# Two graph-attention layers on one core: the order of the first group's work, and the last batch's store

## The chip, the core and the metric

The kernel runs on one core of a Trainium2 chip. A core has five engines that run beside each other and meet at semaphores: TensorE (PE, matrix products; its weight loads, PEld, are shown apart), VectorE (DVE), ScalarE (ACT), GpSimd (POOL) and SyncE (SP, which here issues the DMAs). The time is device microseconds (us) of one execution. It is given as a median over runs, and a profile of one execution shows where it goes.

## What is computed

The input `x` has 64 batches of 256 nodes with 512 features, in float32, and there is one 256 x 256 adjacency. Two layers follow, each with a norm in front and a residual behind:

```
h = relu(layernorm(x))
H = h @ W                                  # 512 -> 256
e = leaky_relu(H @ a[0] + (H @ a[1]).T, 0.2), masked by adj
x = x + concat(softmax(e) @ H, H)
h = relu(layernorm(x))
q, k, v = h @ WqT + bq, h @ WkT + bk, h @ WvT + bv     # 8 heads of 64
p = softmax(mask(q k^T / 8));   x = x + (p @ v) @ WoT + bo
```

## The kernel before

**Groups and steps.** The batches are worked in 32 groups (`g`) of two batches (`b`). Three groups are in hand at once, in stages written as Python generators. Each `next()` on a generator emits one piece of its stage. `first_norm(g)` computes the norm in front of layer 0 and turns its result into `hT0`; `first_layer(g)` is layer 0 and the second norm, which ends in `hT` and its sums; `project(g)` makes q, k and v; `scores`, `mask_pairs`, `weigh` and `outputs` are the attention of one batch. The norm's result is turned by PE for group 0. For the others DVE transposes blocks into `xt`, a DMA writes them to DRAM (`passed`), four more bring them back (`moved`), and `put` copies them into place on ACT.

**Products.** `project` and `outputs` use seven half-size products in place of eight. A product's operand can be a sum of quarters: `operand_sums` makes the sums of the data on POOL (`sums`), `weight_sums(name)` (L254) those of a weight, with four subtractions on DVE. In `project` each of q, k and v has seven pieces; the first, third and fourth product are copied from PSUM into `kept` tiles, the last into place, all by `take` (L686) on ACT, and DVE adds the others. A product that continues in the same bank can start only when the copy has read it.

**The written order.** A planner orders each engine's instructions by their dependencies and its own estimate of time. Where the text wants more, it draws edges that bind only the order on one engine: `after(instruction, name)` (L115), and `not_sooner` (L123), which puts an operation behind the one that was last written for its engine. PE's whole order is the order of the text. `take` draws such an edge for groups 0 and 1, behind whatever was last written for ACT.

**The first group.** Before the loop over groups a hand-written stretch fills the pipeline. One string (L890) gives, for each of the last nineteen of project(0)'s twenty-one pieces, numbered i = 2 to 20, what else is emitted behind it: n a piece of `first_norm`, s a piece of `first_layer(1)`. After these, each i also takes one piece of `judge()` (L283), the check that decides whether this version's bounds on the inputs hold. `judge` squares and sums weights on ACT (`squares`, L328), sums over the partitions with one product on PE (`total`), raises to powers on POOL (`norm`) and compares with small DVE operations (`test`); its verdict `wrong` is read into registers by every engine (L51). `weight_sums` comes at i = 2 (k), 8 (v) and 19 (o).

**The steps.** Each batch of each group then has a string of parts (L906, and L914 for the very first): S is its scores, m a masked head pair, u a piece of `project(g + 1)`, s of `first_layer(g + 2)`, n of `first_norm`, o of `outputs` of the batch before. In the very first step there is no batch before, and o emits nothing. At three quarters of the string `value_differences` is emitted (POOL), at half of it the residual's bias and the load of a later batch. `weigh` of a batch comes at the start of the next step.

**The end.** `outputs` adds seven products into quarters of `xt`, one DVE addition each, and then issues one store of the batch (L847).

Of the kernel before, what the change touches and what calls it, by code (L numbers as in the profile page):

```python
# [10 lines left out]
AF = mybir.ActivationFunctionType  # L11
# [46 lines left out]
def bounded(  # L58
# [224 lines left out]
    def judge():  # L283

        part = const.tile([P, 10], F32, name="part")
        vector.memset(part, 0.0)
        room = att.tile([P, 2 * HP + 1, P], F32, tag="p", name="room", bufs=1)  # L290
        heads = room[:, 2 * HP, :]
        vector.memset(heads, 0.0)
        for j in range(2):
            vector.memset(heads[j * DH : (j + 1) * DH, j * DH : (j + 1) * DH], 1.0)
        power = {}

        def bank(name):
            return mm(name).rearrange("p (h o) -> p h o", h=HP)

        for n, name in enumerate(("q", "k")):  # L300
            gram = bank(f"gram_{name}")
            for hp in range(HP):
                half, cols = hp // 2, slice(hp % 2 * P, (hp % 2 + 1) * P)
                for c in range(HP):
                    w = w_sb[name][:, c % 2, c // 2 * 2 + half, cols]
                    matmul(gram[:, hp, :], w, w, start=(c == 0), stop=(c == HP - 1))
            power[name] = room[:, n * HP : (n + 1) * HP, :]
            vector.tensor_mul(
                power[name], gram, heads[:, None, :].to_broadcast([P, HP, P])
            )  # L310
            yield
        for i in range(3):
            for n, name in enumerate(("q", "k")):
                square = bank(f"square_{name}{i}")
                for hp in range(HP):
                    a = power[name][:, hp, :]
                    matmul(square[:, hp, :], a, a, start=True, stop=True)
                if i < 2:
                    not_sooner(scalar, "copy", power[name], square)
                else:  # L320
                    scalar.activation(
                        power[name], square, AF.Square, accum_out=part[:, 8 + n : 9 + n]
                    )
                yield

        room = big.tile([P, D], F32, tag="oT1", name="squares", bufs=1)

        def squares(col, *srcs):  # L328
            sums = small.tile([P, HP], F32, tag="sums", name=f"sums{col}", bufs=2)
            for i, src in enumerate(srcs):  # L330
                to = room[:, : src.free_size()]
                if len(src.shape) == 3:
                    to = to.rearrange("p (a b) -> p a b", a=src.shape[1])
                not_sooner(
                    scalar, "activation", to, src, AF.Square, accum_out=sums[:, i : i + 1]
                )
                if src.free_size() == D and i < HP - 1:
                    yield
            vector.reduce_sum(part[:, col : col + 1], sums[:, : len(srcs)], axis=AX.X)

        yield from squares(3, *[w_sb["v"][:, :, i, :] for i in range(HP)])
        yield
        for i in range(2):
            yield from squares(i, w0_sb[:, :, i])
        yield from squares(4, bcol["q"])
        yield from squares(5, bcol["k"])
        yield from squares(6, bv_col)
        vector.reduce_max(part[:, 7:8], bad.rearrange("p a t -> p (a t)"), axis=AX.X)
        yield
        yield from squares(2, *[w0_sb[:, c, 2:] for c in range(HP)])  # L350
        yield
        for _ in range(3):
            yield
        total = mm("total")[:, :10]
        matmul(total, square_ones, part, start=True, stop=True)
        norm = const.tile([P, 10], F32, name="norm")
        vector.tensor_scalar(norm, total, 1e-30, None, op0=ALU.add)
        power = const.tile([P, 10], F32, name="power")
        gpsimd.memset(power, 0.5)
        gpsimd.memset(power[:, 7:8], 1.0)  # L360
        gpsimd.memset(power[:, 8:10], 1.0 / 32)
        gpsimd.tensor_tensor(norm, norm, power, op=ALU.pow)
        yield
        root = float(D) ** 0.5

        test = const.tile([P, 5], F32, name="test")
        side = const.tile([P, 2], F32, name="side")
        vector.tensor_add(test[:, 0:1], norm[:, 0:1], norm[:, 1:2])
        vector.tensor_scalar(
            test[:, 0:1], test[:, 0:1], root / LARGEST_SCORE, None, op0=ALU.mult  # L370
        )
        vector.tensor_scalar(side, norm[:, 8:10], root, None, op0=ALU.mult)
        vector.tensor_add(side, side, norm[:, 4:6])
        vector.tensor_mul(test[:, 1:2], side[:, 0:1], side[:, 1:2])
        vector.tensor_scalar(
            test[:, 1:2], test[:, 1:2], scale / LARGEST_SCORE, None, op0=ALU.mult
        )
        vector.tensor_scalar(
            test[:, 2:3], norm[:, 2:3], root / LARGEST_VALUE, None, op0=ALU.mult
        )  # L380
        vector.scalar_tensor_tensor(
            test[:, 3:4], norm[:, 3:4], root, norm[:, 6:7], op0=ALU.mult, op1=ALU.add
        )
        vector.tensor_scalar(
            test[:, 3:4], test[:, 3:4], 1.0 / LARGEST_VALUE, None, op0=ALU.mult
        )
        vector.tensor_scalar(test[:, 4:5], norm[:, 7:8], 2.0, None, op0=ALU.mult)
        vector.tensor_scalar(test, test, 1.0, None, op0=ALU.is_le)
        held = const.tile([P, 1], F32, name="held")
        vector.tensor_reduce(held, test, axis=AX.X, op=ALU.min)  # L390
        vector.tensor_scalar(wrong, held[0:1, :], -1.0, 1.0, op0=ALU.mult, op1=ALU.add)
        yield
# [4 lines left out]
    def stats(mv, src, t, name):  # L397
        st = small.tile([P, 6], F32, tag="st", name=f"st{name}_{t}", bufs=4)
        if vector.last:
            not_sooner(vector, "bn_stats", st, src[t])  # L400
        else:
            vector.bn_stats(st, src[t])
        vector.bn_aggr(mv[:, t, :], st)

    def norm_T(src, mv, name, by_pe):

# [16 lines left out]
        def norm(b):  # L423
            less, rstd = factor[b]
            for t in range(NT):
                r = b * NT + t
                xn[r] = att.tile([P, D], F32, tag="xn", name=f"xn{name}_{r}", bufs=2)
                operands = dict(bias=less[:, t : t + 1], scale=rstd[:, t : t + 1])
                if scalar.last:
                    not_sooner(scalar, "activation", xn[r], src[r], AF.Relu, **operands)  # L430
                else:
                    scalar.activation(xn[r], src[r], AF.Relu, **operands)

# [30 lines left out]
        def put(b, dst):  # L464
            for t in range(NT):
                to = dst[:, :, t * P : (t + 1) * P]
                if not by_pe:
                    to = to.rearrange("p c (i n) -> p c i n", n=S)
                not_sooner(scalar, "copy", to, turned[b * NT + t])

        return factors, norm, turn, fetch, put

# [63 lines left out]
    def first_layer(g):  # L536
# [99 lines left out]
            yield  # L636
        put(1, hT[:, :, N:])
        operand_sums(gpsimd, quads, sums)
        yield

    def residual(g):
# [16 lines left out]
    def project(g):  # L658
        ops = operands.pop(g)
        for name in ("q", "k", "v"):  # L660
# [24 lines left out]

            def take(to, bank, half):  # L686

                behind = [scalar.last] if g <= 1 else []
                if name == "v":
                    taken = [scalar.copy(to, bank)]  # L690
                else:
# [46 lines left out]
    def scores(g, b):  # L738
# [6 lines left out]
        for i in range(HP):  # L745
# [7 lines left out]
                    )  # L753
            pair = p[:, 2 * i : 2 * i + 2]
            for j in range(2):
                not_sooner(scalar, "activation", pair[:, j], sc[j], AF.Exp, scale=scale)
        places.extend((q_tag, k_tag))
        return p

    def mask_pairs(p):  # L760

        for i in range(HP):
# [1 line left out]
            not_sooner(  # L764
                vector, "tensor_mul", pair, pair, maskT[:, None, :, :].to_broadcast([P, 2, NT, N])
            )
            not_sooner(
                gpsimd, "tensor_add", pair[:, :, 0, :], pair[:, :, 0, :], pair[:, :, 1, :]
            )
            yield  # L770

    oTs = {}
# [36 lines left out]
    def outputs(g, b):  # L809
# [31 lines left out]
        yield  # L841
        product(second, 4, False)
        add(1, 0, second)
        yield
        product(first, 3, False)
        add(0, 1, first)
        nc.sync.dma_start(og[g, b], xt)  # L847
        yield


# [39 lines left out]
    order = "n - - - - - nss s s ss ss s s n n sn - s n".split()  # L890
    for i, parts in enumerate(order, 2):
        next(products)
        if i in (2, 8, 19):
            weight_sums("kvo"[i // 7])
        for part in parts:
            if part != "-":
                next(norms if part == "n" else pieces, None)
# [10 lines left out]
    for g in range(NG):  # L908
        products = project(g + 1) if g + 1 < NG else iter(())
        pieces = first_layer(g + 2) if g + 2 < NG else iter(())  # L910
        for b, parts in enumerate(steps):
            if g == b == 0:

                parts = "Smmnn" + parts[4:].replace("uumon", "uumnon", 1)  # L914
            if waiting is not None:
                weigh(*waiting)
                late = outputs(*waiting[:2])
            for i, part in enumerate(parts):
# [13 lines left out]
                if i == (len(parts) * 3 // 4, 6)[b]:  # L932
                    value_differences(g, b)
                if i == len(parts) // 2:
                    if b == 0 and g + 1 < NG:
                        residual(g + 1)
                    if g + 3 < NG:
# [376 lines left out]
```

## Time and profile before

| | |
|---|---|
| median of 3 runs | 2494.8 us (2494.15 to 2494.99) |
| the profiled execution | 2494.22 us; span from first to last instruction 2492.5 us, mean granted PE clock 0.998 |
| busy in the span | PE 2456.6 us (99%), PEld 2041.8 (82%), DVE 1684.7 (68%), ACT 1010.8 (41%), POOL 1017.6 (41%) |
| chain of work that ended last | PE 95%, DVE 2%, DMA 1%, ACT 1%, issue 1% |
| stores of the output | 64 of 512 KB, issued by SP; median 3.1 us from issue to landing |
| last DVE addition into the output | 2486.78 to 2487.20 us |

Such a profile comes from one execution. In rows of instructions in order of time, the first number is the start in us, the second the length; then engine, line, operation, the tile written and the tile read (a name stands for all tiles of that name), and the shapes. A bracket at the end tells how long the engine had been idle and what released it. Most operations carry L35, the line of the helper that records them, so one goes by the tiles' names: `kept_v` is a copy of v's products, `hT<-moved` is `put`, `xn` the norm's application, `r` the reciprocals of the softmax sums, `po` layer 0's weighted sum, `pq`, `pk`, `pv` the projections, `py` the output products.

### The profile page before, as it was taken

The numbers are of one execution on the slowest core, as the hardware profiler recorded it, in microseconds if no ns is written. First come the engines' busy times: TensorE is split into PE (matmuls) and PEld (weight loads), VectorE is DVE, ScalarE is ACT, GpSimd is POOL, SyncE is SP. The second block draws the span as 40 slices with busy tenths as digits, with TensorE's granted clock in tenths as the row PEclk, the third lists the DMA queues.
The fourth block names the chain that finished last, engine by engine and source line by source line (L and its number), as shares of the span: only waits on it lengthen the run. The fifth ranks groups of instructions, "written<-read, shape, count | busy, mean of one in ns | idle before, by whom it ended". The sixth has DMA issues, their size and how long they took to land.

```text
span 2492.5 us, 41319 instructions
## 1 busy us (share of the span) xinstructions
PE 2456.6 (99%) x16034; PEld 2041.8 (82%) x16034; DVE 1684.7 (68%) x3002; ACT 1010.8 (41%) x2019; POOL 1017.6 (41%) x978
## 2 busy tenths in 40 slices
PE   8899999999999999999999999999999999999998
PEld 7678888888888888888888888888888888888886
DVE  6576666767667767667766667676677666676656
ACT  5443443434443434434444344344444344343321
POOL 3433444334444334443344443344433444433332
PEclk9999999999999999999999999999999999999999
DMA  6221232322222222323222323223222223232100
GB/s 190 72 89 64 73 106 77 106 79 77 87 92 91 95 78 75 101 81 102 79 86 78 100 83 106 79 70 94 87 96 87 83 73 106 80 103 79 58 26 36
DMA packets 134809, 213.58 MB, mean 86 GB/s; under 512 B 15440, under 2 KB 79696, under 8 KB 134608
## 3 DMA queue, kind: packets, MB, share of 16 engines
q1 hardware_dynamic: 134608, 210.89, 26.3%
q8 instruction: 128, 2.10, 0.4%
q14 instruction: 73, 0.60, 0.1%
HBM read 112.20 MB, written 98.63 MB: 85 GB/s over the span
## 4 chain that ended last, share of the span: by engine, by line
PE 95%; DVE 2%; DMA 1%; ACT 1%; issue 1%; POOL 0%; SPq 0%; ACTq 0%; DVEq 0%; POOLq 0%
PE pq L137 16%; PE py L137 15%; PE pk L137 15%; PE pv L137 15%; PE sc L137 10%; PE ph L137 9%; PE pr L137 8%; PE po L137 4%; PE total L137 3%; DMA moved<-passed 0%; DVE p L35 0%; DVE r L35 0%; DMA own<-line 0%; DVE st L35 0%; DMA passed<-xt 0%
## 5 line engine op out<-in xcount | busy, mean ns | idle before, releaser
L35 POOL TENSOR_TENSOR p<-p 128x512 f32<-128x512 f32 x256 | 410.0, 1616 | 711.5 <-DVE p L35 711.5
L35 ACT ACTIVATE p<-sc 128x512 f32<-128x512 f32 x512 | 257.7, 627 | 235.7 <-PE sc L137 231.8
L35 DVE TENSOR_TENSOR p<-p,maskT 128x1024 f32<-128x1024 f32 x256 | 340.9, 1352 | 0.0
L35 DVE TENSOR_TENSOR x<-py,x 128x256 f32<-128x256 f32 x448 | 185.8, 415 | 168.7 <-PE py L137 159.5
L35 ACT ACTIVATE xn<-x,factor 128x512 f32<-128x512 f32 x256 | 194.5, 807 | 223.4 <-POOL factor L35 223.4
L35 DVE RECIPROCAL r<-total 128x256 f32<-128x256 f32 x128 | 215.6, 1726 | 90.9 <-PE total L137 90.9
L137 PE MATMUL py<-wo_sb,oT 128*128 128x256 f32 x1024 | 262.5, 380 | 1.7 <-DVE x L35 1.1
L137 PE MATMUL sc<-q,k 64*128 64x256 f32 x2048 | 252.3, 389 | 1.3 <-DVE r L35 0.8
L137 PEld LDWEIGHTS sc<-q,k 64*128 64x128 f32 x2048 | 211.1, 187 | 43.0 <-issue 26.3
L137 PE MATMUL pk<-hT,wk_sb 128*128 128x256 f32 x1024 | 244.8, 382 | 0.0
L137 PE MATMUL pv<-wv_sb,hT 128*128 128x256 f32 x1024 | 238.6, 381 | 6.0 <-ACT kept_v L35 6.0
L35 POOL TENSOR_TENSOR factor<-factor,rexp 128x2 f32<-128x2 f32 x128 | 91.5, 715 | 364.1 <-DVE factor L35 364.1
L137 PE MATMUL pq<-hT,wq_sb 128*128 128x256 f32 x1024 | 239.9, 382 | 0.0
L137 PE MATMUL ph<-w_sb,hT 128*128 128x258 f32 x1024 | 234.6, 381 | 0.3 <-ACT hT L35 0.3
L137 PE MATMUL pr<-p,v 128*32 128x256 f32 x4096 | 232.7, 379 | 0.0
L137 PEld LDWEIGHTS pv<-wv_sb,hT 128*128 128x128 f32 x1024 | 195.5, 191 | 33.2 <-ACT kept_v L35 6.8
L137 PEld LDWEIGHTS pk<-hT,wk_sb 128*128 128x128 f32 x1024 | 192.4, 190 | 35.4 <-issue 10.7
L137 PEld LDWEIGHTS pq<-hT,wq_sb 128*128 128x128 f32 x1024 | 192.0, 190 | 35.0 <-issue 9.9
L137 PEld LDWEIGHTS ph<-w_sb,hT 128*128 128x128 f32 x1024 | 194.4, 190 | 29.8 <-ACT hT L35 0.9
L137 PEld LDWEIGHTS py<-wo_sb,oT 128*128 128x128 f32 x1024 | 194.4, 190 | 29.4 <-DVE x L35 1.5
L137 PEld LDWEIGHTS pr<-p,v 128*32 128x32 f32 x4096 | 133.4, 110 | 87.6
L137 PE MATMUL py<-wo_sb,o_sums 128*128 128x256 f32 x768 | 197.6, 380 | 3.6 <-DVE x L35 3.6
(124 smaller groups left out, 3640.1 us busy)
## 6 DMA issues: line engine op xcount, KB each, us to landing
passed<-xt SPq DMA_DIRECT2D x124, 512.0 KB, 2.7
moved<-passed SPq DMA_DIRECT2D x496, 128.0 KB, 3.1
x<-in_x_dram SPq DMA_DIRECT2D x64, 512.0 KB, 4.2
out_dram<-x SPq DMA_DIRECT2D x64, 512.0 KB, 3.1
own<-line SPq DMA_DIRECT2D x31, 256.0 KB, 3.0
wq_sb<-in_L_gnn_Wq_dram SPq DMA_DIRECT2D x2, 512.0 KB, 9.3
wk_sb<-in_L_gnn_Wk_dram SPq DMA_DIRECT2D x2, 512.0 KB, 10.8
wv_sb<-in_L_gnn_Wv_dram SPq DMA_DIRECT2D x2, 512.0 KB, 7.5
```

The lines of the kernel that those rows point to most:

```text
L35: instruction = getattr(self.engine, operation)(*args, **kwargs)
L137: in_order(nc.tensor.matmul(*args, **kwargs))
```

## The change

- `judge`: three pieces pass, in place of one, before the squares of layer 0's weight (`squares(2)`), and two, in place of four, between these and `total`. Behind the powers six pieces pass in place of one before the tests, and five of the tests get an edge behind DVE's last written operation.
- `take`: v's copies in groups 0 and 1 get no edge.
- `norm` and the exponentials of the first step (all but the first head pair's) get edges behind the last `put` as well; the masked pairs' additions on POOL get one behind the last `operand_sums`.
- `weight_sums("o")` moves from i = 19 to the middle of the first step. That step's string has no o's, one more u, and two s's stand one u earlier; half and three quarters of it fall at i = 14 and 21, from 17 and 26.
- `outputs` of the last group stores each batch in three parts: row block 1 and the first half of row block 0 one piece earlier, the other half at the end.

```diff
@@ judge
         vector.reduce_max(part[:, 7:8], bad.rearrange("p a t -> p (a t)"), axis=AX.X)
         yield
+        yield
+        yield
         yield from squares(2, *[w0_sb[:, c, 2:] for c in range(HP)])
         yield
-        for _ in range(3):
-            yield
+        yield
         total = mm("total")[:, :10]
...
         gpsimd.tensor_tensor(norm, norm, power, op=ALU.pow)
-        yield
+        for _ in range(6):
+            yield
...
-        vector.tensor_add(test[:, 0:1], norm[:, 0:1], norm[:, 1:2])
+        not_sooner(vector, "tensor_add", test[:, 0:1], norm[:, 0:1], norm[:, 1:2])
...
@@ norm_T
+    put_last, sums_last = [], []
...
-                    not_sooner(scalar, "activation", xn[r], src[r], AF.Relu, **operands)
+                    last = scalar.last
+                    taken = scalar.activation(xn[r], src[r], AF.Relu, **operands)
+                    for other in [last, *put_last]:
+                        after(taken, other)
...
                 not_sooner(scalar, "copy", to, turned[b * NT + t])
+            put_last[:] = [scalar.last]
@@ first_layer
         operand_sums(gpsimd, quads, sums)
+        sums_last[:] = [gpsimd.last]
@@ project, take
-                behind = [scalar.last] if g <= 1 else []
+                behind = [scalar.last] if g <= 1 and name != "v" else []
@@ scores
-                not_sooner(scalar, "activation", pair[:, j], sc[j], AF.Exp, scale=scale)
+                last = scalar.last
+                made = scalar.activation(pair[:, j], sc[j], AF.Exp, scale=scale)
+                for other in [last, *put_last] if g == b == 0 and i else [last]:
+                    after(made, other)
@@ mask_pairs
-            not_sooner(
-                gpsimd, "tensor_add", pair[:, :, 0, :], pair[:, :, 0, :], pair[:, :, 1, :]
-            )
+            last = gpsimd.last
+            made = gpsimd.tensor_add(pair[:, :, 0, :], pair[:, :, 0, :], pair[:, :, 1, :])
+            for other in [last, *sums_last]:
+                after(made, other)
@@ outputs
         product(second, 4, False)
         add(1, 0, second)
+        if g == NG - 1:
+            nc.sync.dma_start(og[g, b][:, 1], xt[:, 1])
+            nc.sync.dma_start(og[g, b][:, 0, : D // 2], xt[:, 0, : D // 2])
         yield
         product(first, 3, False)
         add(0, 1, first)
-        nc.sync.dma_start(og[g, b], xt)
+        if g == NG - 1:
+            nc.sync.dma_start(og[g, b][:, 0, D // 2 :], xt[:, 0, D // 2 :])
+        else:
+            nc.sync.dma_start(og[g, b], xt)
@@ the written order
-        if i in (2, 8, 19):
-            weight_sums("kvo"[i // 7])
+        if i in (2, 8):
+            weight_sums("kv"[i // 7])
...
-                parts = "Smmnn" + parts[4:].replace("uumon", "uumnon", 1)
+                parts = "Smmnnuuuumnnmussnussuunununsu"
...
                 if i == len(parts) // 2:
+                    if g == b == 0:
+                        weight_sums("o")
```

More of the change, by code (lines that the diff above doesn't have):

```diff
@@ L371, in judge @@
         )
-        vector.tensor_scalar(side, norm[:, 8:10], root, None, op0=ALU.mult)
+        not_sooner(vector, "tensor_scalar", side, norm[:, 8:10], root, None, op0=ALU.mult)
         vector.tensor_add(side, side, norm[:, 4:6])
@@ L377, in judge @@
         )
-        vector.tensor_scalar(
+        not_sooner(
+            vector, "tensor_scalar",
             test[:, 2:3], norm[:, 2:3], root / LARGEST_VALUE, None, op0=ALU.mult
         )
-        vector.scalar_tensor_tensor(
+        not_sooner(
+            vector, "scalar_tensor_tensor",
             test[:, 3:4], norm[:, 3:4], root, norm[:, 6:7], op0=ALU.mult, op1=ALU.add
@@ L386, in judge @@
         )
-        vector.tensor_scalar(test[:, 4:5], norm[:, 7:8], 2.0, None, op0=ALU.mult)
+        not_sooner(vector, "tensor_scalar", test[:, 4:5], norm[:, 7:8], 2.0, None, op0=ALU.mult)
         vector.tensor_scalar(test, test, 1.0, None, op0=ALU.is_le)
```

## The prediction

> **What bounds the kernel now.** I read three views in order: busy time in stretches, then what TensorE (PE) waits for in the bad stretches, then ScalarE (ACT) and VectorE (DVE) in order of time at those waits. The first, in columns: stretch, length, busy us of PE, PEld, DVE, ACT, POOL (with instruction counts), granted clock, DMA share, GB/s.
>
> ```profile
> 60.00:80.00 20.00, 16.84 (x63) 12.74 (x62) 9.46 (x23) 8.43 (x30) 1.91 (x2) 0.91 0.04 14
> 80.00:100.00 20.00, 16.36 (x76) 13.70 (x74) 12.62 (x45) 7.83 (x13) 9.57 (x11) 1.00 0.32 105
> 100.00:120.00 20.00, 18.39 (x96) 14.98 (x95) 14.07 (x19) 11.88 (x25) 14.78 (x12) 1.00 0.32 107
> 120.00:140.00 20.00, 19.18 (x162) 14.79 (x161) 12.12 (x22) 10.47 (x22) 8.90 (x10) 1.00 0.11 41
> 160.00:180.00 20.00, 15.02 (x108) 11.08 (x110) 7.79 (x16) 5.23 (x9) 4.07 (x5) 0.91 0.45 136
> 181.00:2440.00 2259.00, 2259.00 (x14756) 1883.16 (x14752) 1531.56 (x2698) 919.81 (x1829) 931.02 (x881) 1.00 0.26 84
> ```
>
> From 181 to 2440 us PE is never idle: nothing in this diff can shorten that. What can be won lies in 57 to 181 us and behind 2487. PE waits there for (us in total, times, longest):
>
> ```profile
> PE pv L137 <- ACT kept_v L35: 8.6, 4, 4.8
> PE po L137 <- DVE e L35: 3.2, 1, 3.2
> PE pq L137 <- POOL sums L35: 1.2, 1, 1.2
> PE sc L137 <- DVE r L35: 0.8, 1, 0.8
> ```
>
> Two of these idle stretches cost more than themselves, as the clock shows (same columns as above):
>
> ```profile
> 71.80:74.90 3.10, 0.00 (x0) 0.00 (x0) 0.85 (x3) 2.84 (x11) 0.00 (x0) 1.00 0.00 0
> 74.90:76.00 1.10, 1.05 (x3) 0.89 (x4) 1.10 (x2) 0.00 (x0) 0.00 (x0) 0.52 0.00 0
> 170.30:172.00 1.70, 1.66 (x4) 1.38 (x5) 0.69 (x1) 0.00 (x0) 0.00 (x0) 0.56 0.00 0
> 174.00:176.00 2.00, 2.00 (x10) 1.76 (x10) 1.98 (x4) 0.00 (x0) 0.00 (x0) 1.00 0.00 0
> ```
>
> After the idle 3.2 and 4.8 us eight matmuls take 3.65 us at half clock; eight at full clock take 1.73 (steps of the chain of waits at 78.60 and 174.88). So each adds 1.92.
>
> **A: squares and tests, 71.8 to 78.6.** DVE masks the attention tile `e` only after it has summed the squares:
>
> ```profile
> 74.05 0.16 DVE L35 TENSOR_REDUCE part<-sums 128x1 f32<-128x4 f32 x1 [2.71 <-ACT squares L35]
> 74.12 1.28 DVE L35 TENSOR_TENSOR e<-e,maskT 128x512 f32<-128x512 f32 x2
> ```
>
> `squares(2)` goes from i=9 to i=11 of the order, so four squarings (0.54 us apart, 2.1 us of ACT) and the reduction no longer stand there. What is late next is the exponential of `e`: its first half ends at 71.20 on ACT, the mask takes 0.67, so `po` starts near 72.0, 0.2 us after PE's last matmul at 71.78. Of 3.17 idle and 1.92 cold, 5.1, 0.2 stay: gain 4.9; I take **4.8**. The moved squares land in ACT's 7.84 us gap ahead of `xn` at 82.58: nothing, or 2.1 us of that chain's slack without the gap. The tests go from i=14 to i=19. Now the first waits 1.35 us on DVE for POOL's power, holding `mv` and `factor` at 86.4. That shortens no PE wait alone; it helps the chain to `hT`. At i=19 the thirteen small operations cost 1.3 to 1.9 us of DVE. SP's read of the verdict (1.0 us, at 89.0) follows them, and `passed` and `moved` DMAs queue behind it; bounded by 0 and 1 us, counted under D.
>
> [...] The rows show the half clock after 3.2 us and 1.92 lost, none after 2.43, so I take 4.8 and 6.9. [...]
>
> **B, C: values' copies in group 0.** The first product's copy is free to start at about 85.5, when eight of the sixteen `pv` matmuls from 83.77 are done, but `take` put it behind `xn`, which waits for POOL:
>
> ```profile
> 87.86 1.52 ACT L35 ACTIVATE xn<-x,factor 128x512 f32<-128x512 f32 x2 [3.04 <-POOL factor L35]
> 89.28 0.56 ACT L35 COPY kept_v<-pv 128x512 f32<-128x512 f32 x1
> ```
>
> PE idles 2.43 us (87.47 to 89.90), and 1.21 more (95.35 to 96.56) where the copy at 95.94 stands behind the next `xn`. Without the edge the planner chooses the order, and no row of these two groups shows it; the bounds are 0 and 3.6. The nearest row is a later group, which has no such edge:
>
> ```profile
> 242.94 0.58 ACT L35 COPY kept_v<-pv 128x512 f32<-128x512 f32 x1 [3.73 <-PE pv L137]
> ```
>
> There ACT stands ready, and PE loses nothing. I take the upper end, **3.6**.
>
> **F: the same in group 1.**
>
> ```profile
> 167.26 1.14 ACT L35 COPY hT<-moved 128x512 f32<-128x512 f32 x2 [3.77 <-DMA moved<-passed]
> 168.30 1.52 ACT L35 ACTIVATE xn<-x,factor 128x512 f32<-128x512 f32 x2
> 169.72 0.56 ACT L35 COPY kept_v<-pv 128x512 f32<-128x512 f32 x1
> ```
>
> The copy waits behind a DMA. PE loses 0.18 at 163.5, then 4.80 and 1.92 cold: 6.9. Late next would be POOL's `sums` for the next projection, which must wait for `hT` (168.4) and for the end of `pv`; but total, pr, sc and two products (1.0 + 3.45 + 3.85 + 3.46 us) come first on PE and cover two sums (2.56). Gain **6.9**, bounds 0 (order kept) and 6.9. The new edges that keep `xn` and the scores' exponentials behind the last `put` restate what the copies' edge implied: 0 where they hold nothing.
>
> **D: output weights' sums.** Four DVE subtractions (2.92 us at 99.20) leave i=19 for the middle of step 0. There they delay `factor` (104.82), hence POOL's `factor` (105.07) and `sums` (107.33), though `hT` is in place at 102.03. PE waits 1.18. Gain **1.2**. In their new place DVE is idle 4.45 us before 120.69 and 4.93 before 126.31, and wo's sums are first used at 152.6. They may take 5.8 us, as wk's did beside busy POOL; without cover that delays `rows`, which the new step order gives two more products of slack.
>
> **E: the step's string.** Dropping the idle o's shifts ss earlier, puts two more products between `rows` and the `e` piece, and moves one product in front of `weigh`. Values' differences move from i=26 to 21, ahead of a `factor`. Now `e`'s leaky step (132.47, 1.49 us) stands ahead of the reciprocals (133.88) on DVE, and PE waits 0.8 for a bank at 137.4; in the later group reciprocals start 1.14 us after total does, and PE doesn't wait. Gain **0.8**, bounds 0 and 0.8.
>
> **Tail.** The last add ends at 2487.20; the 512 KB store is issued at 2487.26, moves its data from 2488.0 to 2489.7 and lands after 3.5 us. With three parts, row 1 (complete at 2486.33) and half of row 0 are issued in the two 0.39 us slots before 2487.2; only 128 KB follow. At the row's 360 GB/s the first 384 KB move from 2487.2 to 2488.3, the last 128 KB end near 2488.7: 1.0 us earlier. [...] I take **0.8**, near the row. A coarse dependency, the last add waiting for the first store to read `xt`, would cost about 3; masks on one pair overlap POOL's adds on another of the same tile `p` (2447 to 2456), which speaks against it.
>
> **Given back.** Pulled some ten us forward, PE reaches work that hangs on DMA round trips. Group 1's `hT`: transposes, 2.6 us `passed`, then `moved` and its copies some 4.6 us after the first issue. By my chain it comes at 92 to 95, its second sum at 97 to 98.5, while PE wants it at 99.0. Group 2's second `put` took 13.0 us from `xn` (107.41) to its end (120.4); `xn` moves to about 97, so it ends at 109.5 to 110.5 against a need at 109.4. And all but the first exponentials stay behind `hT`'s second copy. Bounds 0 and 5.1 (a 3.2 us wait with its cold spell); since only one of these slacks is negative, I take **1.5**.
>
> **Sum.** 4.8 + 3.6 + 6.9 + 1.2 + 0.8 + 0.8 = 18.1, minus 1.5 = 16.6. The profiled execution took 2494.2 (its span 2492.5 and 1.7 around it): 2477.6. The median shown lies 0.6 above: **2478.2**.
>
> **Rivals.**
> - R1, the planner keeps group 0's copies behind `xn` anyway: 3.6 less, 2481.8. For it: both are ready within 2 us of each other. Against: the later groups.
> - R2, the `hT` round trips of the pulled-forward stage become a wait long enough for a cold spell: 5.1 instead of 1.5, 2481.8 too, or 2483 with POOL's `factor` ahead of `sums`.
> - R3, the change doesn't do what it says in group 1: the copy stays behind the DMA'd `put`. Without F, B and C: 16.6 - 10.5 = 6.1, 2488.7.
> - R4, slower: `norm`'s new edge stands in all groups, not two. If `xn` then waits in every group behind a `put` whose DMA is late, PE stalls once a group. With the 0.8 us of the smallest bank wait times 31 groups, 24.8 - 16.6 = 8.2 slower: 2503.0. It decides from 16.6/31 = 0.54 us a group. Against it: in steady groups the last ACT instruction before such an `xn` already follows that `put`, often by a whole product.
>
> **Chances.** Forecast 0.62, R1 0.13, R2 0.15, R3 0.06, R4 0.04. A measurement of this kernel tells 0.2% (5.0 us) from no change. All but R4 and a corner of R3 lie beyond it: faster 0.93, same 0.03, slower 0.04. All terms in full give 2476.7; the 0.9 us of small waits near 59 and 103, A at 4.9 and the tail at 1.0 could go too, 1.2 together: low 2475.2. R1 and R2 reach 2483, and both partly 2485: high 2485. That leaves R3 and R4 out.
>
> **What would show it.** In the changed trace: (A) no half clock near 75 and `po` within 0.3 us of the matmul before it; (B, C, F) `kept_v` starting within 0.5 us of its product, no PE wait on it; (D) no PE wait on POOL `sums`; (E) none on `r`; PE idle between 20 and 175 below 4 us, from 14.7; last store landing 0.8 sooner. Wrong would be a cold spell between 85 and 115, any PE idle in the steady groups, or `xn` waiting for `put` there.

## The result, and the profile after

The changed kernel takes 2488.82 us (median of 12 runs, 2487.74 to 2489.48) beside 2494.76 for the kernel before on the same chip (12 runs, 2493.7 to 2495.39): ratio 0.9976, 95% interval 0.9967 to 0.9985. It is faster by 5.9 us. The forecast was 2478.2, a gain of 16.6, and its range ended at 2485.0, so the time lies 3.8 us outside it. The profiled execution's span is 2486.4 us.

The same stretches as before, in the changed kernel (columns as in the prediction):

```profile
60.00:80.00 20.00, 20.00 (x85) 15.77 (x86) 13.34 (x37) 9.38 (x32) 2.89 (x5) 1.00 0.04 14
80.00:100.00 20.00, 15.29 (x81) 12.65 (x79) 14.49 (x39) 9.08 (x17) 9.45 (x11) 0.97 0.39 131
100.00:120.00 20.00, 18.38 (x77) 15.36 (x78) 10.46 (x12) 10.85 (x22) 15.86 (x12) 0.86 0.26 81
120.00:140.00 20.00, 20.00 (x167) 15.88 (x166) 13.59 (x23) 11.84 (x26) 6.36 (x8) 1.00 0.11 41
160.00:180.00 20.00, 18.00 (x150) 13.46 (x149) 13.31 (x21) 8.16 (x15) 6.85 (x6) 0.94 0.41 124
181.00:2430.00 2249.00, 2249.00 (x14694) 1872.10 (x14693) 1525.17 (x2687) 915.20 (x1820) 928.53 (x880) 1.00 0.26 84
```

The gap at 72 us is gone, and from 181 us on PE is as full as before. But 80 to 120 us is no better: PE is idle for 6.3 us there (5.3 before), and the clock, 1.00 before, is 0.97 and then 0.86. The waits of PE from 20 to 185 us (us in total, times, longest) name one main cause, which before held PE once, for 0.4 us:

```profile
PE sc L137 <- ACT p L35: 8.3, 3, 5.9
PE ph L137 <- ACT hT L35: 0.3, 1, 0.3
```

All waits on `kept_v`, `e`, `sums` and `r` are gone. In their place PE's scores wait for exponentials to free a bank (a part of PSUM, where products are written), three times. Two of these waits (5.94 and 2.00 us) are followed by half clock (a granted clock of 0.50 from 101.6 to 105 and from 177.5 to 180.5 us). They are loss 1 and loss 2 below.

**Loss 1, at 95 us.** PE in order of time in the changed kernel (start, length, then what is done; the bracket tells idle time and releaser):

```profile
91.65 2.94 PE L137 MATMUL sc<-q,k 64*128 64x256 f32 x24
94.99 0.70 PE L137 MATMUL sc<-q,k 64*128 64x256 f32 x2 [0.40 <-ACT p L35]
101.62 2.07 PE L137 MATMUL sc<-q,k 64*128 64x256 f32 x6 [5.94 <-ACT p L35]
103.63 4.76 PE L137 MATMUL pq<-hT,wq_sb 128*128 128x256 f32 x16
```

PE reaches the scores at 91.65, 8.6 us sooner than before (100.21), and then stands. Sixteen `pq` products took 3.72 us before (at 105.09, clock 1.00) and take 4.76 here, at a mean clock of 0.78. ACT in the same stretch shows what stood in front of the exponentials `p`:

```profile
94.34 0.60 ACT L35 ACTIVATE p<-sc 128x512 f32<-128x512 f32 x1
99.94 1.14 ACT L35 COPY hT<-moved 128x512 f32<-128x512 f32 x2 [5.00 <-DMA moved<-passed]
100.98 2.54 ACT L35 ACTIVATE p<-sc 128x512 f32<-128x512 f32 x5
```

ACT is idle for 5.00 us, held by the last `put`, whose data are not there. One step further back, SP's issues (first view) and its waits from 84 to 110 us (second view):

```profile
86.82 0.38 SPq L35 DMA_DIRECT2D passed<-xt  x1
95.21 1.74 SPq L466 DMA_DIRECT2D moved<-passed  x4
```

```profile
SPq L466 <- DMA passed<-xt: 7.8, 3, 3.3
SPq L51 <- DVE wrong L35: 7.1, 1, 7.1
```

Between `passed` and its four `moved` SP issues nothing for 8 us. For 7.1 us it stands at L51, the read of the verdict. In the kernel before the same pair of DMAs and the same wait were:

```profile
93.19 0.34 SPq L35 DMA_DIRECT2D passed<-xt  x1
96.29 1.73 SPq L457 DMA_DIRECT2D moved<-passed  x4
```

```profile
SPq L51 <- DVE wrong L35: 0.6, 1, 0.6
```

The verdict itself comes late, from DVE:

```profile
90.64 0.86 DVE L35 TENSOR_TENSOR test<-norm 128x1 f32<-128x1 f32 x1
91.53 0.15 DVE L35 TENSOR_SCALAR test<-test 128x1 f32<-128x1 f32 x1
91.60 1.13 DVE L35 TENSOR_SCALAR side<-norm 128x2 f32<-128x2 f32 x1
...
94.12 0.14 DVE L35 TENSOR_SCALAR wrong<-held 1x1 int32<-1x1 f32 x1
```

So the chain reads: tests at i = 19, verdict at 94.26, SP's read, `moved` at 95.21, `put` at 99.94, exponentials at 100.98, scores at 101.62.

**Loss 2, at 174 us.** ACT, then PE, in order of time:

```profile
171.79 1.08 ACT L35 ACTIVATE p<-sc 128x512 f32<-128x512 f32 x2 [5.85 <-PE sc L137]
172.76 1.14 ACT L35 COPY hT<-moved 128x512 f32<-128x512 f32 x2
173.79 1.52 ACT L35 ACTIVATE xn<-x,factor 128x512 f32<-128x512 f32 x2
175.21 3.02 ACT L35 ACTIVATE p<-sc 128x512 f32<-128x512 f32 x6
```

```profile
175.85 1.13 PE L137 MATMUL sc<-q,k 64*128 64x256 f32 x6 [2.00 <-ACT p L35]
176.91 5.41 PE L137 MATMUL pq<-hT,wq_sb 128*128 128x256 f32 x16
```

In group 1 the planner has put a `put` and an `xn`, 2.45 us together, between the first and the other exponentials. PE waits 2.00 us, and the sixteen products behind these scores run at half clock for the most part (mean clock 0.68): 5.41 us, where the full-clock pace is 3.46.

**Where the time went.** The starts of four landmarks on PE and of the last DVE addition cut each trace into parts: the first `gram_q`; `total`, the product in `judge`; the last `pr` but one, and the last `pr` (the attention's products with v). What lies before `gram_q` is loading, no experiment changes it, and it varied from 21.96 to 23.54 us between runs. "Middle" is from `total` to the last `pr` but one.

| kernel | to `gram_q` | `gram_q` to `total` | middle | `pr` to `pr` | to last add | to the end |
|---|---|---|---|---|---|---|
| before | 21.96 | 61.67 | 2374.76 | 17.51 | 10.88 | 5.72 |
| changed | 22.40 | 56.85 | 2372.90 | 17.51 | 10.88 | 5.86 |

The first 80 us gain 4.82. The middle gains 1.86, where the prediction had 12.5 and took 1.5 off. The end gains nothing. (The first `gram_q` starts 0.44 us later in this trace, which no edit explains.)

### The profile page after: what moved, and what is told of

It is laid out like the page before. It is cut to its first block, busy times and chain, and to the rows that moved or that the text cites. A ratio compares the mean times of both kernels' runs of the same rounds, so it can differ in the third digit from the quotient of the medians.

```text
span 2486.4 us, 41322 instructions
## 1 busy us (share of the span) xinstructions
PE 2456.1 (99%) x16034; PEld 2039.9 (82%) x16034; DVE 1687.1 (68%) x3002; ACT 1011.4 (41%) x2019; POOL 1017.3 (41%) x978
## 4 chain that ended last, share of the span: by engine, by line
PE 97%; DVE 1%; DMA 0%; ACT 0%; issue 0%; SPq 0%; ACTq 0%; DVEq 0%
PE pq L137 16%; PE pk L137 16%; PE pv L137 15%; PE py L137 15%; PE sc L137 10%; PE ph L137 9%; PE pr L137 9%; PE po L137 4%; PE total L137 3%; DVE p L35 0%; DMA w_sb<-in_L_gnn_W_dram 0%; DVE r L35 0%; PE gram_q L137 0%; PE gram_k L137 0%; DVE prod L35 0%
```

## The experiments

Two theories stood. **V**: loss 1 is the verdict, which holds `moved` back in SP's queue. **P**: loss 2 is the order on ACT that the freed copy of v opened, with `put` and `xn` between exponentials. Rivals for loss 1 were the new edge that ties the exponentials to `put`, and the DVE time of the tests themselves. Times are medians, with the kernel before on the same chip beside them or close by (2494.76 to 2495.76). The brackets hold the ratio to that kernel and its 95% interval. Where a version's runs scatter by 2 us, the middle part of its trace decides; it comes from one trace for each version, and a spell of half clock more or less moves it by up to 2 us, so such spells are named.

### The tests early again

```diff
-        for _ in range(6):
-            yield
+        yield
         root = float(D) ** 0.5
```

> The changed kernel, but with one piece between the powers and the tests, as before, in place of six. Theory V (the verdict's read on SP stands ahead of four moved DMAs and waits for the moved tests): the read no longer waits, the DMAs go out at about 89.6 us in place of 95.2, the 5.9 us wait of the scores' matmuls and the slow clock behind it go, and the time falls from 2488.8 to 2480 to 2483 us. Rival T (the DMA round trip is late by itself once its work is pulled forward): no more than 1 us of change, 2488 to 2489.

2481.18 us (ratio 0.9945, 0.9928 to 0.9962), 7.6 less than the changed kernel; middle 2366.35, 6.55 less. SP in order of time:

```profile
86.99 0.38 SPq L35 DMA_DIRECT2D passed<-xt  x1
90.65 1.74 SPq L465 DMA_DIRECT2D moved<-passed  x4
```

`moved` follows `passed` after 3.7 us instead of 8.4. The long wait for an exponential is gone (0.8 us is left of it); loss 2 is still there, with its 2.0 us and a clock of 0.83 from 170 to 180. V is right about the place. Whether by SP's read or by DVE's time, this run does not tell.

### The tests late, their verdict later

```diff
-        vector.tensor_scalar(wrong, held[0:1, :], -1.0, 1.0, op0=ALU.mult, op1=ALU.add)
+        last_word.append(held)
...
+            if g == 2 and b == 0:
+                not_sooner(
+                    vector, "tensor_scalar", wrong, last_word[0][0:1, :], -1.0, 1.0,
+                    op0=ALU.mult, op1=ALU.add,
+                )
```

> The changed kernel with its tests where the change puts them, but the one-element operation that writes the verdict is moved to the start of group 2, so that SP's read goes there too. Theory V: the DMAs go out at about 89.6 us and the time falls to 2480 to 2483 us, as with early tests. Rival D (the tests' own time on VectorE, some 3.5 us from 90.6 to 94.3, delays what follows): the tests are still there, so no gain, 2487 to 2489. Rival T: 2488 to 2489.

2483.22 us (0.9953, 0.9937 to 0.997); middle 2367.18, 5.72 less than the changed kernel. The tests keep their place and their DVE time (90.79 to 94.23), only the verdict is written later, SP's read of it goes to 254.9, and `moved` goes out at 90.62. Loss 2 and its half clock are still there (0.83 from 170 to 180). The other engines read the verdict too, but in the changed kernel none of them before 2459.7, so their reads cannot be what held the first group. So 5.7 of loss 1's 6.55 us are SP's read. The other 0.8 goes with the tests' late place; that it is their time on DVE is likely, but no run isolates it.

### The first exponentials without the new edge

```diff
-                for other in [last, *put_last] if g == b == 0 and i else [last]:
+                for other in [last]:
```

> The changed kernel without the new edge that keeps the first step's exponentials behind the last hT copy. Rival E (this edge makes the wait): the scores' matmuls no longer wait 5.9 us and the time falls to 2480 to 2483 us. Theory V: the hT copy is still late, so the wait only moves from the scores to the third q product, which needs the sums of hT; 2486.5 to 2489 us.

2486.21 us (0.997, 0.9958 to 0.9981); middle 2368.30, 4.60 less. PE's waits from 20 to 185 us:

```profile
PE pq L137 <- POOL sums L35: 3.6, 1, 3.6
PE sc L137 <- ACT p L35: 2.4, 2, 2.0
```

The scores flow, but `hT` is as late as in the changed kernel (`moved` at 96.12), and PE waits for its sums sixteen `pq` matmuls later, again with half clock behind (0.83 from 100 to 110 us). The wait stays without the edge, so the edge is not its cause. Not all of the 4.60 us belongs to it either, because loss 2 is cheaper here: after the same wait, PE runs at full clock (1.00 from 170 to 180 us).

```profile
173.86 1.13 PE L137 MATMUL sc<-q,k 64*128 64x256 f32 x6 [2.00 <-ACT p L35]
174.92 3.72 PE L137 MATMUL pq<-hT,wq_sb 128*128 128x256 f32 x16
```

That is 1.7 us (3.72 in place of 5.41) which the edit does not explain. About 2.9 us are left by which the edge makes the late `hT` dearer: it stops PE some twenty matmuls sooner.

### Group 1's first exponentials behind the last put

```diff
-                for other in [last, *put_last] if g == b == 0 and i else [last]:
+                for other in [last, *put_last] if (g == b == 0 and i) or (g == 1 and b == 0) else [last]:
```

> The changed kernel, with the exponentials of group 1's first step put behind the last hT copy as well, so that this copy and the norm's two applications stand ahead of all eight exponentials. Theory P (the second loss, near 172 to 182 us, comes from their place between the exponentials once v's last copy is free): the wait of 2.0 us and the slow q products behind it go, and the time falls by 3 to 4.5 us, to 2484.3 to 2486 us. Rival T (the copy's data arrives late): no change, or a longer wait ahead of the first exponential, 2488 to 2491.

2484.57 us (0.9959, 0.9945 to 0.9973); middle 2369.04, 3.86 less. ACT:

```profile
167.51 1.52 ACT L35 ACTIVATE xn<-x,factor 128x512 f32<-128x512 f32 x2
172.37 4.03 ACT L35 ACTIVATE p<-sc 128x512 f32<-128x512 f32 x8 [3.33 <-PE sc L137]
```

All eight exponentials run in one stretch, PE is full from 170 to 180 us at clock 1.00. P is confirmed. The `put` and the `xn` had not been waiting for data: it was the order alone.

### Both mended

The first and the fourth edit together.

> Both repairs on the changed kernel: the tests one piece after the powers, and group 1's first exponentials behind the last hT copy. If the two losses are separate (theories V and P), their gains add: 2481.2 of the first alone less 4.2 of the second, 2476 to 2478.5 us. If the second was only an echo of the first, it stays at 2480 to 2482 us.

2477.33 us (0.9927, 0.9914 to 0.9941), five runs between 2476.91 and 2479.67: the lowest median of all. The middle is 2362.19, 10.71 less than in the changed kernel; the two single gains add to 10.41. PE's waits for exponentials are down to 1.2 us, 0.8 the longest.

### Both mended, parts of the change undone

Each of these is the version above with one more edit, so its cost is what that part of the change is worth.

**One store again:**

```diff
-        if g == NG - 1:
-
-            nc.sync.dma_start(og[g, b][:, 1], xt[:, 1])
-            nc.sync.dma_start(og[g, b][:, 0, : D // 2], xt[:, 0, : D // 2])
...
-        if g == NG - 1:
-            nc.sync.dma_start(og[g, b][:, 0, D // 2 :], xt[:, 0, D // 2 :])
-        else:
-            nc.sync.dma_start(og[g, b], xt)
+        nc.sync.dma_start(og[g, b], xt)
```

> As with both repairs, but the last group's batches are stored in one piece again. Theory S (a store of 128 KB in rows of 1 KB lands no sooner after the last addition than one of 512 KB): the same time as with three parts, within 0.4 us. The forecast's rival: 0.8 us slower than with three parts.

2477.63 us (0.9928, 0.9914 to 0.9942), 0.3 more; from the last addition's start to the end 5.72 us, with the split 5.34. Among the twelve traces with the split this part ranges from 5.27 to 5.92 (mean 5.56), so no gain is shown that is clear of this spread.

**Values' copies held as before:**

```diff
-                behind = [scalar.last] if g <= 1 and name != "v" else []
+                behind = [scalar.last] if g <= 1 else []
```

> As with both repairs, but v's copies stand behind ACT's last written work again. If the forecast's terms B, C and F are sized right, the 3.6 and 6.9 us come back: 10.5 us slower than with both repairs, near 2487.5 us. If later waits take part of it up, 5 to 9 us slower.

2483.41 us (0.9951, 0.9937 to 0.9965), 6.1 more; middle 6.45 more. PE's waits:

```profile
PE pv L137 <- ACT kept_v L35: 5.7, 3, 2.6
```

Three of the four waits come back, but shorter than the 8.6 us of before (the longest 2.6, not 4.8, again with a spell of half clock: 0.91 from 160 to 170 us). In group 1 the held copy now follows the `put` (155.80) directly; before, an `xn` of 1.5 us stood between them.

**Squares back in their old place:**

```diff
         yield
-        yield
-        yield
         yield from squares(2, *[w0_sb[:, c, 2:] for c in range(HP)])
         yield
-        yield
+        for _ in range(3):
+            yield
```

> As with both repairs, but the squares of layer 0's weight are back ahead of the mask of e, the tests staying where they are. If term A is sized right: 4.8 us slower than with both repairs, with the idle 3.2 us and the slow clock near 75 us back. If the pulled-forward stage only waits for its hT copies instead, 1 to 3 us slower.

2486.31 us (0.9962, 0.9949 to 0.9976), 9.0 more, where term A says 4.8. `gram_q` to `total` is 4.26 longer: the 2.9 us and the half clock of A are back (0.83 from 70 to 80 us). The rest is a second wait, again with half clock in part (0.83 from 100 to 110 us):

```profile
PE po L137 <- DVE e L35: 2.9, 1, 2.9
PE pv L137 <- DVE v L35: 2.7, 1, 2.7
```

Now five of the thirteen tests fall beside POOL's residual adds (91.82 to 96.75 us). Four of these take 1.08 to 1.18 us each, the eight behind the adds 0.14 to 0.17, and v's additions stand behind them all on DVE. So the tests' cost here went with what POOL did at their date (5.9 us of DVE, beside 2.9 with the tests early), and moving the squares moved that date.

**Output weights' sums back at i = 19:**

```diff
-        if i in (2, 8):
-            weight_sums("kv"[i // 7])
+        if i in (2, 8, 19):
+            weight_sums("kvo"[i // 7])
...
-                    if g == b == 0:
-                        weight_sums("o")
```

> The best version so far, with the output weights' four subtractions back at place 19 of the first group's order, ahead of group 1's normalisation factors on DVE. The prediction's term D says that moving them gained 1.2 us: so 2478.5, with a wait of PE for POOL's sums of 1.2 us. Rival: the operations around them on DVE now have other neighbours (POOL's residual adds no longer run beside them), so that nothing is late: 2477.3. Third: as with the squares, one idle stretch long enough for a half clock follows: 2480 or more.

2479.86 us (0.9938, 0.9925 to 0.9952); middle 1.68 more. PE's wait for `sums` is back, at 1.4 us, which is term D.

**The step's string as before:**

```diff
-                parts = "Smmnnuuuumnnmussnussuunununsu"
+                parts = "Smmnn" + parts[4:].replace("uumon", "uumnon", 1)
```

> The best version so far, with the order string of group 0's first step as it was before. The prediction's term E says that the new string gained 0.8 us: so 2478.1, with PE waiting 0.8 us for the reciprocals r between 130 and 145. Rival: the old string's wait hung on the output weights' sums and value differences in their old places and does not come back: 2477.3. Third: the old string puts e's pieces so early that a longer wait with a half clock comes: 2480 or more.

2478.97 us (0.9937, 0.9923 to 0.995); middle 1.13 more. PE's waits:

```profile
PE sc L137 <- DVE r L35: 0.6, 1, 0.6
```

That is term E's wait at its place (129.8 us).

### Two attempts to gain more

**Both mended, group 0's exponentials free:**

```diff
-                for other in [last, *put_last] if (g == b == 0 and i) or (g == 1 and b == 0) else [last]:
+                for other in [last, *put_last] if g == 1 and b == 0 else [last]:
```

> The best version so far (tests early, group 1's first exponentials behind the last put), with group 0's first exponentials no longer behind the last put. In the best version PE still waits 1.2 us in two pieces for an exponential between 90 and 100 us. Theory: the put edge costs that wait and nothing else, so 1.2 us at most go: 2476.1 beside 2477.3, no half clock. Rival, as in the run without this edge on the changed kernel: POOL's pair additions then run ahead of the sums of hT, and PE waits for sums instead: 2477.3 or up to 1 us more.

2479.73 us (0.9937, 0.9924 to 0.9951); middle 1.43 more. The waits for exponentials fall from 1.2 to 0.4 us, and one of 1.4 us for POOL's `sums` takes their place. The rival is right: once `moved` is on time, the change's edge in group 0 earns 1.4 us, where with the late `moved` it cost some 2.9.

**Both mended, verdict later** (the edit of the second experiment on top):

> The best version so far, with the operation that writes the verdict moved to the start of group 2, so that SP's read of it stands behind no transfer of group 1. If the theory of SP's queue is complete, the early tests have taken the whole cost away already and nothing is left to gain: 2477.3 within 0.5, moved issued at the same time within 0.2 us. Rival: the read still costs its own 1 us ahead of passed or moved: 2476.3, with moved issued 1 us sooner.

2479.47 us (0.9934, 0.9921 to 0.9948); middle 0.19 less, `moved` at 91.82 in place of 91.87. With the tests early, SP's read costs nothing measurable, so nothing of V is left over.

The medians of the last four stand 1.6 to 2.5 us above 2477.33, more than their middles say. Two things outside of the middle, told below under the hardware, move single traces by as much, so these four are judged by their middles.

## Why the prediction was wrong

| part of the prediction | forecast | measured | by |
|---|---|---|---|
| A, squares and tests | 4.8 | 4.82 | `gram_q` to `total`, before to changed |
| B, C, F, D, E before "given back" | 12.5 | 12.57 | middle, before to both mended |
| given back | -1.5 | -10.71 | middle, changed to both mended |
| the last store | 0.8 | -0.1 | last add to the end |

**A** came as worked out: `po` starts at 72.22, no idle, no half clock (1.00 from 60 to 80 us). **B, C and F**: no wait on `kept_v` is left in either group; the planner chose the order that the later group showed. **D** and **E** also hold: undone in the mended version they cost 1.7 and 1.1, forecast 1.2 and 0.8. That the whole group comes to 12.57 of 12.5 is partly luck. Undone one at a time, its parts cost 6.45 (B, C and F, forecast 10.5), 1.68 and 1.13, which is 9.3; and the mended version has one edge, in group 1, that the change lacks.

**The step that failed is "Given back".** It was taken as 1.5 with bounds 0 and 5.1, and measured 10.71, which is what the two repairs win back. It failed in two places of the text.

First, in part A: SP's read of the verdict, with "`passed` and `moved` DMAs queue behind it; bounded by 0 and 1 us, counted under D". The 1 us was the length of the read itself, and D's 1.2 holds nothing for it. What counts is when the value that it reads is ready. The move from i = 14 to i = 19 put the tests at 90.6 us, while the same prediction let everything in front of `hT` come 10 us sooner. The read thus came to stand ahead of a transfer that could have gone out near 90 us (90.65 with the tests early). The price was 5.72 us for SP and 0.8 with the tests' late place. The prediction named the signs (a cold spell between 85 and 115 us) and the rival R2 with the right place, `hT`; it priced R2 as a slack of 3.2 us and looked for its cause in the round trip's own length. The round trip was not the late part: from `moved`'s issue to `put` it took 4.7 us, beside some 4.6 in the text.

Second, in part F: the new edges "restate what the copies' edge implied: 0 where they hold nothing". In group 0 the edge on the exponentials is not 0 either: it made the late `hT` some 2.9 us dearer. In group 1 the exponentials have no such edge; before, the copy's edge behind `put` and `xn` had kept these ahead of the first exponentials (167.26 and 168.30 in the rows that F quotes). Freed, the planner moved them in between: 3.86 us, of which 2.00 is idle and the rest half clock. So F's wait went, as forecast, and 3.9 us were lost again behind it.

**The tail**: the forecast took landing to follow the data, so that 128 KB in place of 512 land sooner. In mid-kernel that is so: the 512 KB store of an earlier batch lands 2.8 us after its issue, and in all twelve traces with the split the last 128 KB of the batch before the final one land after 1.7. At the very end both are slower: the one store takes 3.5 and 3.6 us (two traces), the last 128 KB take 2.9 to 3.5. In the changed kernel the bulk of the data has moved about 1.4 us after the last addition's end, against 2.4 before, as forecast, but a trickle of 10 to 41 GB/s goes on to 2484.0, and the store lands at 2484.5. What slows the last stores is not shown.

R4's edge cost nothing, as argued: PE is full from 181 to 2430. R1 and R3 did not happen. The measured 2488.8 is close to R3's 2488.7, but that is chance: the copies did what the change says. A slip without effect: by its own terms (2476.7 less 1.2) the low end is 2475.5, not 2475.2.

## What to carry to other kernels

- Here the read of a computed value into the registers of SP, which issues the DMAs, was a wait in their queue until the value was written: 7.1 us ahead of a read of 0.48, and `moved` at 95.21 us where it goes out at 90.62 with the read moved away. Price such a read by the date of the value against the dates of the transfers behind it, not by its own length.
- When edges are taken away, ask what order they had produced as a by-product, in each group where they stood, and whether anything else still asks for it. Here one new edge was given to group 0 alone, and group 1 was left without one.
- If a change pulls a stage forward by ten microseconds, list all that must be there at the new date and work out each one's own date under the change. A single lump for "slack" hid the one item that the change itself had moved the other way.

## What the hardware showed that was not expected

**The half clock depends on more than the length of the idle time.** In the kernel before 2.43 us of idle were followed by full clock (1.00 from 89.9 to 92 us); in the changed one 2.00 us were followed by sixteen products in 5.41 us; and the same 2.00 us at the same place, in the run without the exponentials' edge, by the same products in 3.72 us. The end of the last group shows it again: the same two waits are followed by half clock in one run and not in another. PE in the version with both mended, and with the output sums back:

```profile
2455.36 1.13 PE L137 MATMUL py<-wo_sb,o_sums 128*128 128x256 f32 x4 [1.31 <-DVE x L35]
2457.57 2.07 PE L137 MATMUL py<-wo_sb,oT 128*128 128x256 f32 x4 [1.08 <-DVE x L35]
2459.43 1.53 PE L137 MATMUL py<-wo_sb,o_sums 128*128 128x256 f32 x4
```

```profile
2456.91 1.13 PE L137 MATMUL py<-wo_sb,o_sums 128*128 128x256 f32 x4 [1.31 <-DVE x L35]
2459.12 1.13 PE L137 MATMUL py<-wo_sb,oT 128*128 128x256 f32 x4 [1.08 <-DVE x L35]
2460.09 1.03 PE L137 MATMUL py<-wo_sb,o_sums 128*128 128x256 f32 x4
```

The idle times are the same, 1.31 and 1.08; the first version loses 1.4 us more (`pr` to `pr` 18.92 against 17.53), at a mean clock of 0.66 from 2457 to 2462 us, where the other has 1.00. It shows in six of the fourteen traces. What decides between the two was not tried. Together with the 1.6 us by which the first `gram_q` varies, this accounts for differences of 2 us between versions of one family that their edits do not explain.

**Tiny DVE operations beside POOL's adds can take almost as long as one add.** `side<-norm`, 128 x 2, takes 1.13 us at 91.60 in the changed kernel, beside POOL's four adds of 128 x 512 (87.75 to 92.70: 4.95 us, 1.24 each), and 0.16 at 87.03 with the tests early, 0.96 us ahead of the same adds. In these two traces and in the one with the squares in their old place, every test of more than 0.2 us stands beside these adds, and none takes longer than 1.18. Not every test beside them is slow: `test<-test`, 128 x 1, took 0.15 us at 91.53. What makes the difference is not shown. The thirteen tests, most of them 0.15 us long, took 3.6 us of DVE in the changed kernel, 2.9 with the tests early, and 5.9 with the squares in their old place.
